# A gated cross-attention and quantized feed-forward kernel: earlier dequantization, a softmax in large steps, later transposes

## The chip, the cores and the metric

The kernel runs on one core of a Trainium2 chip. The core has a matrix engine (TensorE, PE in the profile, with its weight loads shown as PEld), a vector engine (DVE), a scalar engine (ACT), GpSimd (POOL) and SyncE (SP), which here only issues DMAs. Each engine works through its own instruction stream in order, and semaphores hold an instruction until what it needs is there. The metric is the device time of one execution in microseconds (us). Three runs of the kernel before took 1498.82, 1499.34 and 1502.29 us; the median is 1499.34 us.

## The reference

The input x has 4 sequences of 1024 tokens of 512 numbers; a context has 4 x 64 tokens. Cut to what is computed:

```
x = x + tanh(g_xattn) * attention(layernorm(x), ctx)      # 16 heads of 64, 64 keys,
                                                          # keys after the token's position get -10000
h = act_qdq(layernorm(x))                                 # rounded to 16 bits by one scale over all of h
up   = act_qdq(h @ dequant(w_up).T)                       # 1536 columns
gate = act_qdq(h @ dequant(w_gate).T)
sig  = round(sigmoid(gate) * 65536) / 65536
gate = act_qdq(gate * sig)
o    = act_qdq(gate * up)
x = x + tanh(g_ffn) * (o @ dequant(w_down).T)
```

act_qdq divides by the largest magnitude of the whole tensor, so each of these four scales needs all of its tensor before the first element can be rounded. dequant works on blocks of 32 weights: the largest magnitude of a block divided by 7 is its scale, the weights are divided by it, rounded and multiplied again. All arithmetic is float32.

## The kernel before, in words

The 4096 tokens are 32 tiles of 128 (t = 0 to 31). A tile scheduler orders the instructions of DVE, ACT, POOL and SP by their place in the program and by when it expects them to be ready, and may move one forward where its engine would be idle; `high_priority(SOON)` makes an instruction count as 150 places earlier, and `keep_in_program_order` forbids moving it. In the large stages PE's order is written out by hand (`manual_schedule`). Twenty buffers of 8 KB per partition (`slot`, NS = 20) are shared by everything large.

**Setup (0 to 79 us).** The weights of the attention are loaded and folded: `m_all` (query and key weights with the context, one matrix per sequence) and `vwo` (value and output weights with the context). `score_sums(0)` (L358) makes the sums of `m_all` that a seven-product form of the score multiplication uses: four DVE additions of 128x1024 (L368 to L373). It stands before the loop that makes `vwo` (L509), whose results go from PSUM to SBUF by ACT (L522) and DVE (L524).

**Attention (79 to 588 us).** The loop over pairs of tiles q calls `scores(q + 1)` and `softmax(q + 1)` one pair ahead, and then `attend(t)` for its two tiles. `softmax` takes the maximum of each head (L590, 128x1024), negates it (L591), runs 16 exponentials on ACT, one a head, with the maximum as bias and the sum collected beside it (L594), and multiplies by the reciprocal sum (L599, L600). `attend` transposes the weights on PE (L614), calls `then()`, which does `renormed(t - 4)` (the second layer norm, L636 to L644) and, in the second half, prepares one of twelve 128-row chunks of the gate weights, and multiplies with `vwo` (L620, 16 matmuls). `gate_chunk` (L239) for chunk oc comes at tile 16 + oc * 16 // 12, that is at 16, 17, 18, 20, 21, 22, 24, 25, 26, 28, 29 and 30. It loads the chunk (L208, SP), dequantizes it with six DVE instructions (L211 to L220; `dequantized`), transposes it with four PE instructions (L225) and copies it to `wgT` on ACT (L228; `turned`). Its raw buffers are two. The first DVE instruction of chunks 0 and 1 is kept in program order. From tile 24 on, eight chunks of the up weights are dequantized as well (`w_eu`), and from tile 26 on sums of `wgT` are made (L288 to L291).

**Gate products (590 to 885 us).** 24 units v, each of 28 matmuls in seven products (m1, m5, m2, m6, m7, m4, m3 of `unit_steps`), interleaved so that the last three steps of a unit run among the first four of the next. The gate results go to DRAM (`gate_d`). The down weights are loaded and dequantized here (`wd`).

**Up products (885 to 1181 us).** 24 more units, `at` = 0 to 23, of 12.0 us each. Beside them `gate_integers(n)` turns gate results that are loaded back (`load_gates`, L938, 1 MB a pair) into integers: for each of 48 half units three ACT instructions (L968, L969, L971), one DVE instruction (L973) and a store on SP (L974). `products` multiplies magnitudes (L994 on ACT, L995 on DVE) to find the place of the largest product. After the loop the first operands of the last stage are asked for (`load_early(0)`, L1085, 1 MB and 0.5 MB), the place of the largest product is found and its row read (L1105), and then, in PE's written order, four transposed chunks of the down weights (`down_turned`, each four transposes L225 and one ACT copy L228), m7, three more, m4, m3, and the last five. `half_of_last` takes in the halves of the last unit as they come (L980, L984, L985). Two more `load_early` follow.

**Down products (1197 to 1499 us).** First the two scales (`up` and `o`) are made by a chain of short DVE and POOL instructions (L184 to L203), and a flag `full` (L1162) is read by every engine for a branch (L1165, L1166) around a fallback that does not run. Then `integers` makes the operands: an ACT instruction (L1193), L1197 and L1202 on DVE. PE does 96 matmuls for the first block of tokens (L1344), then the seven-product form for the others (L1267), to the end.

Of the kernel before, what the change touches and what calls it, by code (L numbers as in the profile page):

```python
# [27 lines left out]
def kernel(  # L28
# [71 lines left out]
    SOON = 150  # L100
    NQ = NT // 2
    QPB = TPB // 2

    xf = x.flatten_outer_dims()
    of = out.flatten_outer_dims()
# [97 lines left out]
            nc.vector.tensor_scalar(inv, inv, unit, None, ALU.mult)  # L203
        return s, inv

    def dequantized(pool, src, w, name, in_order=False):
# [4 lines left out]
        ins = nc.vector.tensor_reduce(am, wb, AX.X, ALU.max, apply_absolute_value=True)  # L211
        if in_order:
            tc.keep_in_program_order(ins)
# [6 lines left out]
        nc.vector.tensor_tensor(wb, wb, am.unsqueeze(2).to_broadcast(shape), ALU.mult)  # L220

    def turned(ps, w, dst, in_order=False):

        for j in range(4):
            ins = nc.tensor.transpose(ps[:, j, :], w[:, j * P : (j + 1) * P], ident)  # L225
            if in_order:
                tc.keep_in_program_order(ins)
        nc.scalar.copy(dst, ps)  # L228

    def weight_chunk(pool, psp, src, dst, name, in_order):  # L230
        w = pool.tile([P, H], F32, name=f"w_{name}", tag="wraw")
        dequantized(pool, src, w, name, in_order)
        turned(psp.tile([P, 4, P], F32, name=f"wps_{name}", tag="tr"), w, dst)

    wgT, wuT, wd, wdT, up_chunks = [], [], [], [], []

    def gate_chunk(pool, psp, oc):  # L239
        if oc % 4 == 0:  # L240
            wgT.append(slot([P, HC, 4 * P], f"wgT{oc // 4}"))
        cols = slice((oc % 4) * P, (oc % 4 + 1) * P)
        weight_chunk(
            pool, psp, w_gate[oc * P : (oc + 1) * P, :], wgT[-1][:, :, cols], f"g{oc}", oc < 2
        )

    def up_chunk(psp, w, in_order=False):

        oc = len(up_chunks)
        up_chunks.append(oc)  # L250
        if oc % 4 == 0:
            wuT.append(slot([P, HC, 4 * P], f"wuT{oc // 4}"))
        cols = slice((oc % 4) * P, (oc % 4 + 1) * P)
        ps = psp.tile([P, 4, P], F32, name=f"wps_u{oc}", tag="tr")
        turned(ps, w, wuT[-1][:, :, cols], in_order)

    def down_chunk(pool, k):
        if k % 4 == 0:
# [117 lines left out]
    with tc.tile_pool(name="su", bufs=1) as su, tc.tile_pool(  # L376
# [122 lines left out]
        for b in range(2, B):  # L499
            for k in range(2):  # L500
                nc.gpsimd.dma_start(out=m_d[b][k], in_=m_all[b][k])
        for _ in score_sums(0):
            pass


        for b in range(B):
            vwo.append([slot([P, HP // 2, H], f"vwo{b}_{n}") for n in range(2)])
        load_group(1)
        for a in reversed(range(B // 2)):  # L509
            for hp in range(HP):  # L510
                for b in (2 * a, 2 * a + 1):
                    ps = ps_mm.tile([P, H], F32, name=f"ps_vo{b}_{hp}", tag="mm")
                    for j in range(2):
                        half = slice(j * D, (j + 1) * D)
                        to = j if b % 2 == 0 else 1 - j
                        nc.tensor.matmul(
                            ps[to * D : (to + 1) * D, :], vT[half, hp, b * KL : (b + 1) * KL],
                            wo[hp // 4][half, hp % 4, :], start=True, stop=True,
                        )
                    dst = vwo[b][hp // 4][:, hp % 4, :]  # L520
                    if b % 2 == 0:
                        nc.scalar.copy(dst, ps)  # L522
                    else:
                        nc.vector.tensor_copy(dst, ps)  # L524
                    if b > 1 and hp % 4 == 3:
                        nc.gpsimd.dma_start(out=vwo_d[b][hp // 4], in_=vwo[b][hp // 4])
# [3 lines left out]
    with tc.tile_pool(name="ps_s", bufs=1, space=PSUM) as ps_s, tc.tile_pool(  # L530
# [48 lines left out]
        def softmax(q, e):  # L579

            for i in range(2):
                t = 2 * q + i
                ei = e[:, i]

                if t % TPB == 0:
                    nc.vector.tensor_tensor(
                        ei, ei, cmask.unsqueeze(1).to_broadcast([P, NH, KL]), ALU.add
                    )
                mx = pa.tile([P, NH], F32, name=f"mx{t}", tag="mx")
                nc.vector.tensor_reduce(mx, ei, AX.X, ALU.max)  # L590
                nc.vector.tensor_scalar(mx, mx, -1.0, None, ALU.mult)  # L591
                sm = pa.tile([P, NH], F32, name=f"sm{t}", tag="sm")
                for h in range(NH):
                    nc.scalar.activation(  # L594
                        ei[:, h, :], ei[:, h, :], AF.Exp, bias=mx[:, h : h + 1],
                        accum_out=sm[:, h : h + 1],
                    )
                rs = pa.tile([P, NH], F32, name=f"rs{t}", tag="rs")
                nc.vector.reciprocal(rs, sm)  # L599
                nc.vector.tensor_tensor(  # L600
                    ei, ei, rs.unsqueeze(2).to_broadcast([P, NH, KL]), ALU.mult
                )
# [51 lines left out]

        sg_t, ag, early_up = [], [], []
        last = NT - GRP
        half = NT // 2
        group_stats(pa, 1)
        rstd_of(pa, [(rstd1[:, of_group(1)], mv1[:, of_group(1), 1])], "a1")

# [7 lines left out]
        for q in range(NQ):  # L668
# [19 lines left out]
            for i in range(2):  # L688
                t = 2 * q + i

                def between():
                    if q > 1:
                        renormed(t - GRP)
                    if t >= half:
                        for oc in range(IC):
                            if t - half == oc * (NT - half) // IC:
                                gate_chunk(pa, ps_tr, oc)

                attend(t, e, between)
                if t >= NT - UPB:  # L700
                    ag.append(weight_sums(wgT, sg_t, t - (NT - UPB), "g"))

# [30 lines left out]
    with tc.tile_pool(name="praw", bufs=RAW) as praw, tc.tile_pool(  # L733
# [184 lines left out]
        with tc.tile_pool(name="pc", bufs=2) as pc, tc.tile_pool(  # L918
# [27 lines left out]
            def up_done(r, v, k):  # L946
# [6 lines left out]
                queue = nc.sync if v == order[-1] else nc.scalar  # L953
                queue.dma_start(out=up_d[u], in_=raw[u])

            gsi = {}
            made = []

            def gate_integers(n):


                for j in range(len(made), min(n, NU)):
# [67 lines left out]
            gates = {v: load_gates(v) for v in order[:3]}  # L1030
            for at, v in enumerate(order):
                tp, p = divmod(v, UPB)
                if p == UPB // 2 and at + UPB < NV:
# [39 lines left out]
                if at > 0:  # L1073
# [8 lines left out]
            def load_early(k):  # L1082
                up, gs = slot([P, 2, UW], f"upe{k}"), slot([P, 2, UW], f"gse{k}", I16)
                for dst, src in ((up, up_d), (gs, gsi_d)):
                    nc.sync.dma_start(  # L1085
                        out=dst, in_=src[2 * k : 2 * k + 2].rearrange("u p w -> p u w")
                    )
                return up, gs
# [312 lines left out]
```

## Time and profile before

| what | value |
|---|---|
| median of three runs | 1499.34 us |
| the profiled execution | 1501.24 us |
| its span, first to last instruction | 1499.4 us |
| PE busy | 1445.4 us, 96% |
| DVE busy | 1086.1 us, 72% |
| ACT busy | 643.4 us, 43% |
| POOL busy | 70.8 us, 5% |
| mean granted TensorE clock | 0.990 |
| mean DMA rate | 155 GB/s |

How to read it: a line of the view of waits says which engine and line waited for which, with the total, the number of times and the longest. A line of the timeline gives the start, the duration, the engine and line, output <- inputs, the shape, the number of instructions taken together and, in brackets, how long the engine had been idle and what ended that. A line of the view of stretches gives, for each stretch, the busy time of the engines (with the number of instructions), the granted TensorE clock as a share of full speed, the mean busy share of the DMA engines and their rate. The profiled execution lies 1.9 us above the median of the runs, and 1.84 us of its time lie outside its span.

### The profile page before, as it was taken

Reading aid. Unit: us, or ns where it says so; the run is one execution under the profiler, and the core shown is the slowest. Engines: PE = TensorE matmul, PEld = TensorE weight load, DVE = VectorE, ACT = ScalarE, POOL = GpSimd, SP = SyncE. Lnnn points to the kernel's source line nnn. Section 1 sums busy time; section 2 is a strip of 40 time slices with the busy share of each in tenths; the row PEclk is TensorE's granted clock in tenths of the full one; section 3 lists DMA queues with packets and bytes.
Section 4 is the critical chain, followed back from the end, with each engine's and each line's share of the span. In section 5 each row is a group of like instructions: output and inputs, shape, how many; then the busy total and the mean of one; then the engine's idle time right before and its main releaser. Section 6 shows DMA issues by size and latency. Waiting matters only on the chain. (4 is left out here: it accounts for less than half of the span.)

```text
span 1499.4 us, 14520 instructions
## 1 busy us (share of the span) xinstructions
PE 1445.4 (96%) x4656; PEld 797.1 (53%) x4656; DVE 1086.1 (72%) x1984; ACT 643.4 (43%) x1715; POOL 70.8 (5%) x143
## 2 busy tenths in 40 slices
PE   8989999998999989999999999999999599999999
PEld 6544445444454545444444444444444248888887
DVE  2865657649577887999856558888888797666642
ACT  2455645665456654110000127777787532222200
POOL 0100000000000001000000000000000101111110
PEclk9999999999999999999999999999999899999999
DMA  7521221302122144743322528868583585554321
GB/s 280 221 89 43 78 78 60 141 21 82 57 84 85 36 162 153 282 176 155 126 84 85 178 88 309 334 203 324 207 338 135 183 313 206 182 183 169 140 71 43
DMA packets 71477, 231.69 MB, mean 155 GB/s; under 512 B 7268, under 2 KB 7524, under 8 KB 65892
## 3 DMA queue, kind: packets, MB, share of 16 engines
q1 hardware_dynamic: 46212, 131.09, 24.8%
q0 software_dynamic: 11648, 50.34, 8.7%
q10 hardware_dynamic: 13536, 49.29, 8.2%
q8 instruction: 37, 0.61, 0.2%
q14 instruction: 44, 0.36, 0.1%
HBM read 123.74 MB, written 106.95 MB: 154 GB/s over the span
## 5 line engine op out<-in xcount | busy, mean ns | idle before, releaser
L594 ACT ACTIVATE e<-e,mx 128x64 f32<-128x64 f32 x512 | 170.2, 337 | 14.7 <-DVE mx L591 14.6
L620 PE MATMUL po<-vb,eT 128*128 128x512 f32 x256 | 116.2, 608 | 0.9 <-ACT eT L616 0.9
L620 PE MATMUL po<-vwo,eT 128*128 128x512 f32 x256 | 114.8, 601 | 2.0 <-ACT eT L616 1.7
L594 ACT ACTIVATION_READ_ACCUMULATOR e<-e,mx 128x1 f32 x512 | 97.3, 190 | 0.0
L756 PE MATMUL pqup<-t,wuT 128*128 128x512 f32 x192 | 91.8, 600 | 2.1 <-DVE raw_up L777 0.9
L756 PE MATMUL pqgate<-t,wgT 128*128 128x512 f32 x192 | 90.4, 593 | 0.0
L620 PEld LDWEIGHTS po<-vb,eT 128*128 128x128 f32 x256 | 48.9, 196 | 57.3 <-issue 55.6
L620 PEld LDWEIGHTS po<-vwo,eT 128*128 128x128 f32 x256 | 47.7, 191 | 58.8 <-issue 53.9
L1193 ACT ACTIVATE uie<-upe,inv_up 128x1024 int16<-128x1024 f32 x48 | 53.7, 1145 | 58.4 <-DVE upe L1197 34.3
L772 ACT COPY raw_gate<-ppgate 128x512 f32<-128x512 f32 x24 | 14.0, 585 | 147.8 <-PE ppgate L756 147.8
L1267 PE MATMUL ep<-wdT,upe 128*128 128x256 f32 x336 | 77.1, 379 | 0.0
L1267 PE MATMUL eq<-tw,upe 128*128 128x256 f32 x312 | 72.5, 379 | 0.2 <-DVE c L1289 0.2
L1267 PEld LDWEIGHTS ep<-wdT,upe 128*128 128x128 f32 x336 | 63.8, 190 | 9.1 <-issue 0.5
L552 DVE TENSOR_TENSOR e<-sq,e 128x512 f32<-128x512 f32 x48 | 33.0, 688 | 47.9 <-PE sq L546 47.9
L756 PE MATMUL ppup<-xu,wuT 128*128 128x512 f32 x144 | 67.7, 592 | 0.0
L756 PE MATMUL ppgate<-xh,wgT 128*128 128x512 f32 x144 | 67.7, 592 | 0.0
L1197 DVE SCALAR_TENSOR_TENSOR upe<-uie,inv_o,gse 128x1024 f32<-128x1024 int16 (+1 forms) x50 | 60.8, 1241 | 9.3 <-ACT uie L1193 4.0
L973 DVE SCALAR_TENSOR_TENSOR q<-gi,inv_gs,si 128x1024 int16<-128x1024 int16 x48 | 60.6, 1278 | 5.0 <-ACT si L971 4.9
L1267 PEld LDWEIGHTS eq<-tw,upe 128*128 128x128 f32 x312 | 59.1, 190 | 8.7 <-DVE c L1289 0.6
L756 PEld LDWEIGHTS pqup<-t,wuT 128*128 128x128 f32 x192 | 35.1, 190 | 51.4 <-issue 34.4
L756 PEld LDWEIGHTS pqgate<-t,wgT 128*128 128x128 f32 x192 | 36.2, 190 | 46.4 <-issue 38.5
L884 DVE TENSOR_REDUCE am_gate<-raw_gate 128x1 f32<-128x1024 f32 x48 | 58.2, 1213 | 0.9
(323 smaller groups left out, 2833.8 us busy)
## 6 DMA issues: line engine op xcount, KB each, us to landing
gate_d<-raw_gate ACTq DMA_DIRECT2D x48, 512.0 KB, 2.6
gt<-gate_d SPq DMA_DIRECT2D x48, 512.0 KB, 6.2
upe<-up_d SPq DMA_DIRECT2D x24, 1024.0 KB, 6.2
up_d<-raw_up ACTq DMA_DIRECT2D x46, 512.0 KB, 4.8
gsi_d<-q SPq DMA_DIRECT2D x48, 256.0 KB, 4.1
gse<-gsi_d SPq DMA_DIRECT2D x24, 512.0 KB, 4.8
xg<-in_x_dram SPq DMA_DIRECT2D x8, 1024.0 KB, 5.3
x_d<-xg POOLq DMA_DIRECT2D x32, 256.0 KB, 2.3
```

Source lines behind the costliest of these rows:

```text
L552: nc.vector.tensor_tensor(dst, bank[at], other, add)
L594: nc.scalar.activation(ei[:, h, :], ei[:, h, :], AF.Exp, bias=mx[:, h : h + 1], accum_out=sm[:, h : h + 1],)
L620: nc.tensor.matmul(po, eT[:, hp, :], vwo[b][hp // 4][:, hp % 4, :], start=(hp == 0), stop=(hp == HP - 1),)
L756: nc.tensor.matmul(bank[at], a[k][:, h, :], b[k][:, h, :], start=start and h == 0, stop=h == HC // 2 - 1, skip_group_check=True,)
L772: nc.scalar.copy(r0[:, 0, :], bank["pp"])
L884: nc.vector.tensor_reduce(am_gate[:, u : u + 1], rf, AX.X, ALU.max, apply_absolute_value=True)
L973: nc.vector.scalar_tensor_tensor(gsi[u], gi, c_gs, si, ALU.mult, ALU.mult)
L1193: nc.scalar.activation(ui, up[:, i, :], AF.Copy, scale=inv_u)
L1197: ins = nc.vector.scalar_tensor_tensor(o[:, i, w], ui[:, w], c_o, gs[:, i, w], ALU.mult, ALU.mult)
L1267: nc.tensor.matmul(bank[at], a[u // 2][k][:, u % 2, q % 2, :], w_of[u // 2][k][:, u % 2, :], start=start and u == 0, stop=u == UPB - 1, sk ...
```

## The change

- `score_sums(0)` is emitted between the two halves of the loop that makes `vwo`.
- For the first pair of tiles (q = 0) the softmax subtracts the maximum with one DVE instruction of 128x1024, takes one ACT exponential of 128x1024 and sums with one DVE reduction of 128x1024, in place of the negation and the 16 exponentials. The other 15 pairs are as before.
- A gate chunk is loaded and dequantized after the `attend` that lies three tiles before the one in which it is transposed, in four raw buffers. No instruction of it is kept in program order any more.
- `gate_integers` runs further ahead in the last units. The number of half units made by the end of unit `at` goes from 2 at + 4 to 2 at + 4 + 2 (at - 17): 42 by unit 18, 46 by unit 19 and all 48 by unit 20, where it was 40, 42 and 44, and 48 by unit 22. Gate loads are asked for correspondingly earlier. The last four integer results go to a slot of their own (`last_q`).
- The three `load_early` are emitted with unit 22, with unit 23 and after the row loads; two of their 16-bit operands share a slot.
- Of the twelve transposed chunks of the down weights one comes before m7, one after it, and ten after m3.
- The ACT instruction L984 of `half_of_last` gets the high priority.

```diff
-        for _ in score_sums(0):
-            pass
...
         for a in reversed(range(B // 2)):
+            if a == 0:
+                for _ in score_sums(0):
+                    pass
...
                 mx = pa.tile([P, NH], F32, name=f"mx{t}", tag="mx")
                 nc.vector.tensor_reduce(mx, ei, AX.X, ALU.max)
-                nc.vector.tensor_scalar(mx, mx, -1.0, None, ALU.mult)
                 sm = pa.tile([P, NH], F32, name=f"sm{t}", tag="sm")
-                for h in range(NH):
-                    nc.scalar.activation(
-                        ei[:, h, :], ei[:, h, :], AF.Exp, bias=mx[:, h : h + 1],
-                        accum_out=sm[:, h : h + 1],
+                if q == 0:
+
+                    nc.vector.tensor_tensor(
+                        ei, ei, mx.unsqueeze(2).to_broadcast([P, NH, KL]), ALU.subtract
                     )
+                    nc.scalar.activation(ei, ei, AF.Exp)
+                    nc.vector.tensor_reduce(sm, ei, AX.X, ALU.add)
+                else:
...
+        gate_at = [NT // 2 + oc * (NT // 2) // IC for oc in range(IC)]
+        gate_raw = {}
...
-                    if t >= half:
-                        for oc in range(IC):
-                            if t - half == oc * (NT - half) // IC:
-                                gate_chunk(pa, ps_tr, oc)
+                    if t in gate_at:
+                        oc = gate_at.index(t)
+                        turned_chunk(ps_tr, gate_raw.pop(oc), oc, wgT, "g")
 
                 attend(t, e, between)
+                if t + AHEAD in gate_at:
+                    oc = gate_at.index(t + AHEAD)
+                    w = pa.tile([P, H], F32, name=f"w_g{oc}", tag="wraw", bufs=4)
+                    dequantized(pa, w_gate[oc * P : (oc + 1) * P, :], w, f"g{oc}")
+                    gate_raw[oc] = w
...
-                    gsi[u] = pc.tile([P, UW], I16, name=f"q{u}", tag="q", bufs=5)
+                    if j < NU - 4:
+                        gsi[u] = pc.tile([P, UW], I16, name=f"q{u}", tag="q", bufs=5)
+                    else:
+                        if j == NU - 4:
+                            last_q.append(slot([P, 4, UW], "last_q", I16))
+                        gsi[u] = last_q[0][:, j - NU + 4]
...
-                nc.scalar.activation(ar, r, AF.Abs)
+                with tc.high_priority(SOON):
+                    nc.scalar.activation(ar, r, AF.Abs)
...
-                    gate_integers(2 * at + min(4, at // 4))
-                    if at + 2 < NV:
-                        gates[order[at + 2]] = load_gates(order[at + 2])
+
+                    late = max(0, at - (NV - UPB - 1))
+                    soon = max(0, at + 1 - (NV - UPB - 1))
+                    gate_integers(2 * at + min(4, at // 4) + 2 * late)
+                    for v in order[len(gates_loaded) : at + 3 + 2 * soon]:
+                        gates_loaded.append(v)
+                        gates[v] = load_gates(v)
+                    if at + 2 >= NV:
+                        load_early()
...
-            early = [load_early(0)]
...
+            load_early()
+
             turn = down_turned(ps_tr)
-            for _ in range(4):
-                next(turn)
+            next(turn)
             half_of_last(0, 0)
-            for step, half, n in zip(tail, ((1, 1), (0, 1), (1, 0)), (3, 0, 5)):
+            for step, half, n in zip(tail, ((1, 1), (0, 1), (1, 0)), (1, 0, IC - 2)):
                 step()
                 half_of_last(*half)
                 for _ in range(n):
                     next(turn)
-            for k in range(1, UPB // 2):
-                early.append(load_early(k))
```

More of the change, by code (lines that the diff above doesn't have):

```diff
@@ L102 @@
     QPB = TPB // 2
+    AHEAD = 3
     xf = x.flatten_outer_dims()
@@ L204, in act_scale, with dequantized @@
         return s, inv
-    def dequantized(pool, src, w, name, in_order=False):
+    def dequantized(pool, src, w, name):
         nc.sync.dma_start(out=w, in_=src)
@@ L210, in dequantized @@
         am = pool.tile([P, NQB], F32, name=f"wam_{name}", tag="wam")
-        ins = nc.vector.tensor_reduce(am, wb, AX.X, ALU.max, apply_absolute_value=True)
-        if in_order:
-            tc.keep_in_program_order(ins)
+        nc.vector.tensor_reduce(am, wb, AX.X, ALU.max, apply_absolute_value=True)
         nc.vector.tensor_scalar(am, am, 1.0 / W_QMAX, 1e-12, ALU.mult, ALU.max)
@@ L220, in dequantized, with turned, turned_chunk, up_chunk @@
         nc.vector.tensor_tensor(wb, wb, am.unsqueeze(2).to_broadcast(shape), ALU.mult)
-    def turned(ps, w, dst, in_order=False):
+    def turned(ps, w, dst):
         for j in range(4):
-            ins = nc.tensor.transpose(ps[:, j, :], w[:, j * P : (j + 1) * P], ident)
-            if in_order:
-                tc.keep_in_program_order(ins)
+            nc.tensor.transpose(ps[:, j, :], w[:, j * P : (j + 1) * P], ident)
         nc.scalar.copy(dst, ps)
[L230 to L233, printed above, removed]
     wgT, wuT, wd, wdT, up_chunks = [], [], [], [], []
-    def gate_chunk(pool, psp, oc):
+    def turned_chunk(psp, w, oc, into, name):
         if oc % 4 == 0:
-            wgT.append(slot([P, HC, 4 * P], f"wgT{oc // 4}"))
+            into.append(slot([P, HC, 4 * P], f"w{name}T{oc // 4}"))
         cols = slice((oc % 4) * P, (oc % 4 + 1) * P)
[L243 to L247, printed above, removed]
+        ps = psp.tile([P, 4, P], F32, name=f"wps_{name}{oc}", tag="tr")
+        turned(ps, w, into[-1][:, :, cols])
+    def up_chunk(psp, w):
         oc = len(up_chunks)
         up_chunks.append(oc)
[L251 to L255, printed above, removed]
+        turned_chunk(psp, w, oc, wuT, "u")
     def down_chunk(pool, k):
@@ L590, in softmax @@
                 nc.vector.tensor_reduce(mx, ei, AX.X, ALU.max)
-                nc.vector.tensor_scalar(mx, mx, -1.0, None, ALU.mult)
                 sm = pa.tile([P, NH], F32, name=f"sm{t}", tag="sm")
-                for h in range(NH):
-                    nc.scalar.activation(
-                        ei[:, h, :], ei[:, h, :], AF.Exp, bias=mx[:, h : h + 1],
-                        accum_out=sm[:, h : h + 1],
-                    )
+                if q == 0:
+                    nc.vector.tensor_tensor(
+                        ei, ei, mx.unsqueeze(2).to_broadcast([P, NH, KL]), ALU.subtract
+                    )
+                    nc.scalar.activation(ei, ei, AF.Exp)
+                    nc.vector.tensor_reduce(sm, ei, AX.X, ALU.add)
+                else:
+                    nc.vector.tensor_scalar(mx, mx, -1.0, None, ALU.mult)
+                    for h in range(NH):
+                        nc.scalar.activation(
+                            ei[:, h, :], ei[:, h, :], AF.Exp, bias=mx[:, h : h + 1],
+                            accum_out=sm[:, h : h + 1],
+                        )
                 rs = pa.tile([P, NH], F32, name=f"rs{t}", tag="rs")
@@ L656 @@
         last = NT - GRP
-        half = NT // 2
+        gate_at = [NT // 2 + oc * (NT // 2) // IC for oc in range(IC)]
+        gate_raw = {}
         group_stats(pa, 1)
@@ L954, in up_done, with load_early @@
                 queue.dma_start(out=up_d[u], in_=raw[u])
+            early = []
+            def load_early():
+                k = len(early)
+                up = slot([P, 2, UW], f"upe{k}")
+                if k % 2 == 0:
+                    early_gs.append(slot([P, 2, 2, UW], f"gse{k}", I16))
+                gs = early_gs[-1][:, k % 2]
+                for dst, src in ((up, up_d), (gs, gsi_d)):
+                    nc.sync.dma_start(
+                        out=dst, in_=src[2 * k : 2 * k + 2].rearrange("u p w -> p u w")
+                    )
+                early.append((up, gs))
+            early_gs, last_q = [], []
             gsi = {}
@@ L1029 @@
             tokens = {done_last: b}
-            gates = {v: load_gates(v) for v in order[:3]}
+            gates_loaded = order[:3]
+            gates = {v: load_gates(v) for v in gates_loaded}
             for at, v in enumerate(order):
@@ L1077 @@
                     products(order[at - 1])
-                    gate_integers(2 * at + min(4, at // 4))
-                    if at + 2 < NV:
-                        gates[order[at + 2]] = load_gates(order[at + 2])
[L1082 to L1088, printed above, removed]
-            early = [load_early(0)]
+                    late = max(0, at - (NV - UPB - 1))
[6 more added lines that the diff above has]
+                        load_early()
             first = over_all([am_p], "first")
```

## The prediction

> **What bounds the kernel now.** I began with the page's busy times.
>
> ```profile
> PE 1445.4 (96%) x4656; PEld 797.1 (53%) x4656; DVE 1086.1 (72%) x1984; ACT 643.4 (43%) x1715; POOL 70.8 (5%) x143
> ```
>
> PE is the bound; no edit removes one of its products. What can be won is its 54 us of idle time (1499.4 - 1445.4), and what each pause costs afterwards. So next came PE's own waits.
>
> ```profile
> PE ps_d L1344 <- DVE upe L1202: 13.0, 1, 13.0
> PE wps_g L225 <- DVE w_g L220: 12.2, 2, 6.8
> ...
> PE ps_e L614 <- DVE e L600: 3.1, 1, 3.1
> PE po L620 <- ACT eT L616: 2.6, 9, 0.5
> PE wps_d L225 <- ACT wdT L228: 2.6, 4, 1.8
> PE ps_vo L516 <- DVE vwo L524: 2.3, 3, 0.9
> ```
>
> All but one of these lie where the change works: the end of the up products, two gate chunks, the first softmax, the copies of `vwo`. Then the timeline, for the price after a pause:
>
> ```profile
> 109.01 1.94 PE L614 MATMUL ps_e<-ident,e 128*128 128x128 f32 x8 [3.06 <-DVE e L600]
> ...
> 110.78 7.76 PE L620 MATMUL po<-vwo,eT 128*128 128x512 f32 x16
> ...
> 356.74 1.09 PE L225 MATMUL wps_g<-ident,w_g 128*128 128x128 f32 x4 [6.77 <-DVE w_g L220]
> ...
> 357.62 8.84 PE L620 MATMUL po<-vb,eT 128*128 128x512 f32 x16
> ...
> 368.07 7.03 PE L620 MATMUL po<-vb,eT 128*128 128x512 f32 x16
> ```
>
> The same 16 products take 7.03 us without a pause and 8.84 after one. The stretches show why: the granted clock is halved.
>
> ```profile
> 355.00:360.00 5.00, 3.26 (x7) 1.93 (x8) 4.97 (x14) 5.00 (x32) 0.00 (x0) 0.50 0.21 56
> ```
>
> Of 5 us PE is busy 3.26, PEld 1.93, DVE 4.97, ACT 5.00, POOL 0; then the clock, 0.50, the DMA share and the rate. So a removed pause brings its length and its aftermath.
>
> Last, the timeline behind the last up product:
>
> ```profile
> 1179.38 1.88 PE L756 MATMUL pnup<-b,su 128*128 128x512 f32 x4
> ...
> 1184.55 0.59 ACT L228 COPY wdT<-wps_d 128x512 f32<-128x512 f32 x1 [0.26 <-PE wps_d L225]
> ...
> 1188.38 0.22 DVE L1162 SCALAR_TENSOR_TENSOR full<-a_ends,other_end,below 128x1 int32<-128x1 f32 x1
> ...
> 1192.56 3.23 ACT L1193 ACTIVATE uie<-upe,inv_up 128x1024 int16<-128x1024 f32 x3 [7.42 <-DMA upe<-up_d]
> ```
>
> The product ends at 1181.26, its scales are ready at 1188.6, ACT starts at 1192.56, 4.0 after the flag, and PE at 1197.54. The chain of waits names DVE from there to 1258, then PE to the end, so what moves ACT's start moves the end.
>
> **Sums of `m_all` (L368 to L373), moved.** Four instructions of 1.22, 4.9 us of DVE, now fill 58.4 to 63.7, in front of the first `vwo` copies. PE's waits on those copies are 2.3, and 0.9 more at the first score product. Behind half of them the sums may still be moved forward into the same gap. Ends: 3.2 gained; 2.5 lost, half of the 4.9 falling between copies with five PSUM buffers as cover. I take 1.0 gained.
>
> **First softmax.** Per tile a negation (0.17) and 16 exponentials (0.33 apart) go; a subtraction (as L600, 1.22), an exponential (as L971, 128x1024, 1.05) and a sum (as L590, 1.17) come. The first maximum is ready at 96.1. Then 1.22, the table load 1.28, 1.05, 1.17, 0.25 (L599) and 1.22 (L600) end at 102.3; the second maximum and the L552 of the next scores lie between, 1.17 + 3 x 0.69, so about 105.5. It was 108.87, and PE wants it at 105.95. The pause of 3.06 goes, and its aftermath: 1.94 - 1.04 on the transposes and 7.76 - 7.03 on the products, 4.7 in all. DVE gets 2 x (1.22 + 1.17 - 0.17) = 4.4 more in a stretch where it is busy 17.1 of 25, so a new wait of 1 is likely. Ends: 4.7 and 0 (if the second tile's 2.4 goes first); I take 3.7.
>
> **Gate chunks.** A chunk is 0.68 + 0.17 + 0.25 + 0.69 + 0.42 + 0.69 = 2.9 us of DVE; its number is unchanged. Tiles 16 to 30 take 208.8 us (357.62 to 566.39 in L620), 14.9 each, so three tiles earlier is some 45 us earlier. Chunk 0, tile 16: the wait of 6.77 goes, and 8.84 - 7.03 and 1.09 - 0.63 behind it: 9.0. Chunk 10, tile 29: a wait of 5.40 and 8.54 - 7.03 and 0.46: 7.4. Late next: at tile 17 the `xm` that DVE makes at 357.65, which PE would want at 358.4, but 5.8 us of chunks 0 and 1 no longer stand before it; at tile 30 the weights whose L600 ends at 552.6, which PE would want at 557. The cover is DVE's free time; at 475 to 500 it is busy 24.89 of 25. The density there stays (gate chunks 9 to 11 replace 7 to 9), so I take off 0.4: 16.0 gained. Ends: 16.4; 9.0, if the second wait is only handed on.
>
> On SP a chunk's load stands behind x and `m_all` loads; with four buffers its buffer is free since the tile five or six before. A new danger: chunks 0 and 1 were loaded at 17.49 already, landing after up to 12.2, but their first DVE instruction was held. Now four chunks are free to go ahead, and DVE, in order, would stand at a load. If that is in front of the copy L460 at 24.77, four landings to about 31 (0.25 MB each at 347 GB/s) and one chunk's 2.9 make 34, 9.4 lost, with 1.6 of slow clock 11. Other end: 3 gained, from work taken off tiles 16 to 20. Nearest row: the ten chunks that were not held cost DVE 2.9 for loads altogether. I take 1.0 lost.
>
> **Gate integers ahead.** Units 18 and 19 each get two half units more: on ACT 2 x (1.14 + 1.14 + 1.05) = 6.7, where it is busy about 9.6 of 12.0 (19 to 21 of 25 in the stretches there). So 4.3 too much, twice, until units 21 and 22, which have none. DVE gets 2.6 on 10.5. Queued behind L968 on ACT are the copies L764 and L772, which PE waits for. SP's stores and loads keep their number; the last gate load is already issued at 1106.6, in unit 18. Ends: 8.6 lost; 0.5 gained by ease later. Nearest row: from 625 to 700 DVE is full and PE does not wait. I take 1.0 lost.
>
> **Behind the last product.** Of seven transposed chunks ahead of m3 two stay: 20 transposes at 0.13 are 2.6, the waits there are 2.95. So m3 could end 5.5 earlier; DVE must still take up m7 (L782) before m4, about 1, so 4.5. L973 no longer stands there (2 x 1.28 off DVE). L984 ahead of the copies saves 0.35. Against: ten chunks then follow, on ACT two each 1.45 apart; five ended 3.9 after m3, ten end 7.5 after, at 1184.3, and the flag comes at 1183.8: 0.5 lost. The `load_early` move before the row load on SP; the third follows it. The 3 MB that fill the DMA engines from 1185 to 1193 go, while ACT passes the branch in 4.0; at the first branch, with the DMA at a fifth, it took 2.3. Ends: 8 gained (with 1.7 of that and the DVE order, L1197 ahead of L1202 by 1.28); 2 lost, if a load holds SP in front of the row load. I take 4.5.
>
> A rule against it: the transposes now stand where PE is otherwise idle. Here the clock is 1.00 until 1186, two microseconds after the last transpose and five after the last product, so the row cannot say which counts. The Trainium skill, "TensorE: Matmul & The Clock Gate", Part 4: PE-mode transpose, says that transposes do not count as PE activity in the same way. By it half of the ten chunks would run at half clock, the copies would end some 2 us later, and this part would be 2.5, the total 2 us more.
>
> **Sum.** -1.0 - 3.7 - 16.0 + 1.0 + 1.0 - 4.5 = -23.2. The profiled execution took 1501.24 (span 1499.4), so 1478.0; from the median, 1499.34, it is 1476.1. I take 1477.
>
> **Rivals.**
> - *Start block* (above): 10 more than I took, 1487. For it, the loads at 17.49; against, DVE's gaps of 3.2 between 31 and 43, in which a chunk fits. 0.13.
> - *The second gate wait handed on* in the full stretch of DVE: 7 more, 1484. For it 24.89 of 25; against, the 5.8 that leave 545 to 562. 0.12.
> - *ACT the bound in units 18 to 20*: 7.6 more, 1485. 0.12.
> - *Nothing won behind the last product*, ACT's copies or the branch taking the 4.5: 1481.5. 0.10.
> - *Slower: every chunk waits for its load.* SP, in order behind a held x load, issues each load only as DVE reaches it; DVE stands 2.8 (median landing) and PE with it, 5.7 with the chunk's 2.9. It outweighs 23.2 + 4.5 from five chunks on; at eight it is 45.6, so 1523. For it, two such waits now (2.9 in all); against, the 45 us ahead. Eight chunks 0.08; four, which give 1500, 0.04.
> - The forecast itself: 0.41.
>
> **How the numbers follow.** About 0.3%, 4.5 us, is what a measurement here can tell from no change. Slower 0.08; the same 0.04; faster 0.88, the forecast and four rivals. Since several of these could meet, I move 0.03 from faster to each side: 0.82, 0.07, 0.11. The low end is all best ends of the known parts, -3.2 - 4.7 - 16.4 - 8 = -32, softened by the 2 of likely cost: 1469. The high end takes in the start block and one further rival: 1494.
>
> **What the new profile would show.** The waits on `w_g` and on L600 gone, the clock at 1.00 at 355 and 555 and its drop at 110 gone; L211 of chunk 0 far ahead of tile 13 and no DVE wait at 25; ACT full without PE waiting in units 18 to 20; m3 about 4.5 sooner relative to its unit, and ACT's first L1193 as much. Wrong it would be by a DVE wait for `w_g` before 50 us, by a wait on `raw_up` after 1090, or by ACT's copies ending after the flag.

## The result, and the profile after

The changed kernel takes 1495.37 us (median; 1494.09 to 1496.3) against 1499.6 for the kernel before in the same comparison: a ratio of 0.9969, 95% interval 0.996 to 0.9979. It is 4.2 us faster, where 23 were forecast, and lies 1.4 above the top of the range. The profiled execution took 1494.27 us, its span is 1492.5 (1499.4 before). The two spans differ by 6.9 and not by 4.2, because the profiled execution before lies 1.6 above the median of its runs and the one after 1.1 below. Lines have moved: the copy L460 is now L447, L600 is L596, L764 is L766, L994 is L1018, L984 is L1008, L1193, L1197 and L1202 are L1213, L1217 and L1222. The kernels made from it for the experiments are up to three lines off again; there the names behind the line tell which instruction it is.

The page's busy times after. The work is the same, PE's idle time is 48.0 us in place of 54:

```profile
PE 1444.5 (97%) x4656; PEld 795.4 (53%) x4656; DVE 1087.2 (73%) x1986; ACT 635.6 (43%) x1653; POOL 70.5 (5%) x143
```

The view of waits after, PE's own:

```profile
PE ps_m L465 <- DVE wqT L447: 15.4, 1, 15.4
...
PE ps_d L1364 <- DVE upe L1222: 4.5, 1, 4.5
PE ppup L758 <- ACT raw_up L766: 4.0, 1, 4.0
...
PE ps_vo L504 <- DVE vwo L512: 1.9, 3, 0.6
...
PE ps_e L610 <- DVE e L596: 0.6, 1, 0.6
```

What the prediction saw go is gone or smaller: the 12.2 for the gate weights are gone, the 3.1 for the first softmax are 0.6, the 13.0 before the down products 4.5. Two waits are new, 15.4 at the start and 4.0 in the up products. The stretches of the two old gate waits, and of the new one at 1125, show the granted clock (the figure behind POOL's count; 0.86 in the first two before):

```profile
350.00:375.00 25.00, 24.88 (x88) 13.12 (x87) 24.06 (x54) 15.45 (x58) 1.08 (x2) 1.00 0.25 91
550.00:575.00 25.00, 24.76 (x91) 13.22 (x90) 23.70 (x64) 15.94 (x68) 1.63 (x3) 1.00 0.16 56
1125.00:1150.00 25.00, 21.74 (x46) 9.36 (x47) 20.66 (x26) 22.34 (x24) 0.00 (x0) 0.93 0.50 179
```

To see where the time went I set the starts of the same PE rows side by side in the two timelines, and took the difference from one landmark to the next:

| from, to | start of the last row (end for the flag), before, after | step | forecast |
|---|---|---|---|
| span start, first `vwo` product | 60.72, 76.91 | +16.2 | +1.0 |
| to the first score product (sums of `m_all`) | 79.31, 95.57 | +0.1 | -1.0 |
| to the second tile's transposes (softmax) | 118.37, 131.14 | -3.5 | -3.7 |
| to the last tile's transposes (gate chunks) | 573.26, 569.67 | -16.4 | -16.0 |
| to m2 of the last up unit (gate integers) | 1163.85, 1166.78 | +6.5 | +1.0 |
| to m3 of the last up unit | 1179.38, 1177.60 | -4.7 | -4.5 |
| to the flag `full` | 1188.60, 1186.84 | 0.0 | 0 |
| to the first down product | 1197.54, 1190.40 | -5.4 | 0 |
| to the end of the span | 1499.4, 1492.5 | +0.2 | 0 |
| sum | | -6.9 | -23.2 |

The start, first the copy of `wqT` in the timeline before, then the same stretch after:

```profile
24.77 1.29 DVE L460 COPY wqT<-ps_wq 128x512 f32<-128x512 f32 x2 [17.39 <-PE ps_wq L456]
```

```profile
29.67 0.69 DVE L212 TENSOR_REDUCE wam_g<-w_g 128x16 f32<-128x512 f32 x1 [22.35 <-DMA w_g<-in_L_ffn_w_gate_dram]
...
38.87 0.69 DVE L219 TENSOR_TENSOR w_g<-w_g,wam_g 128x512 f32<-128x512 f32 x1
39.48 1.28 DVE L447 COPY wqT<-ps_wq 128x512 f32<-128x512 f32 x2
40.31 3.48 PE L465 MATMUL ps_m<-kT,wqT 64*128 64x256 f32 x16 [15.40 <-DVE wqT L447]
```

DVE stands from 7.3 to 29.67 at the load of a gate chunk that is not wanted before tile 16, then makes four chunks (24 instructions, 9.8 us), and only then the copy that PE has wanted since 24.9. The first 16 products after it take 3.48 instead of 2.00, as the granted clock is 0.50 from 29.70 to 43.35.

Tile 16, where PE waited 6.77 and took 8.84 for the 16 products:

```profile
362.61 0.66 PE L224 MATMUL wps_g<-ident,w_g 128*128 128x128 f32 x4
363.10 7.03 PE L616 MATMUL po<-vb,eT 128*128 128x512 f32 x16
```

The up products, ACT's and PE's rows in order of time:

```profile
1111.87 2.19 ACT L986 ACTIVATE gi<-gt,inv_gate 128x1024 int16<-128x1024 f32 x2
...
1119.53 2.34 ACT L986 ACTIVATE gi<-gt,inv_gate 128x1024 int16<-128x1024 f32 x2 [0.93 <-DVE q L996]
...
1125.75 1.99 ACT L1018 ACTIVATE ar<-raw_up 128x1024 f32<-128x1024 f32 x2
...
1127.65 0.56 ACT L766 COPY raw_up<-ppup 128x512 f32<-128x512 f32 x1
1128.26 3.30 PE L758 MATMUL ppup<-xu,wuT 128*128 128x512 f32 x4 [3.96 <-ACT raw_up L766]
```

Four half units (two from 1111.87, two from 1119.53) stand on ACT in front of the magnitudes L1018. These two read the raw buffers of unit 18, and the copy L766 of unit 20 writes into one of them. So m2 of unit 20 waits 3.96, and 1.9 more go in slow products (3.30 and 2.31 for 1.88 and 1.88, the clock at 0.50 from 1128.79 to 1132.20).

Behind the flag, in the timeline after:

```profile
1186.62 0.22 DVE L1182 SCALAR_TENSOR_TENSOR full<-a_ends,other_end,below 128x1 int32<-128x1 f32 x1
...
1187.81 4.38 ACT L1213 ACTIVATE uie<-upe,inv_up 128x1024 int16<-128x1024 f32 x4 [1.29 <-SPq L1186]
...
1188.99 0.75 DVE L1217 SCALAR_TENSOR_TENSOR upe<-uie,inv_o,gse 128x512 f32<-128x512 int16 x1 [0.91 <-ACT uie L1213]
...
1189.78 0.52 DVE L1222 TENSOR_SCALAR upe<-upe 128x512 f32<-128x512 f32 x1
...
1190.40 10.00 PE L1364 MATMUL ps_d<-wdT,upe 128*128 128x512 f32 x19 [4.50 <-DVE upe L1222]
```

From the flag to the first down product it is 3.56 now, 8.94 before. The view of the branch's line of the kernel *before* shows that the prediction misread that time:

```profile
L1166 DVEq COMPARE_BRANCH  x1: 63/63/63, 1189.0 to 1189.0; - x1
...
L1166 ACTq COMPARE_BRANCH  x1: 45/45/45, 1193.0 to 1193.0; - x1
```

DVE took the branch at 1189.0, ACT at 1193.0, *after* the start of its first L1193 at 1192.56. So that L1193 stands in front of the branch in ACT's stream, and ACT did not need 4.0 to pass the branch: it stood for something in front of it, and in the changed kernel the first L1213 starts 1.0 after the flag.

What it stood for is in the trace's semaphore updates, and it is not what the bracket of the row names (a load of `upe`). ACT's wait went on until 1192.32. The one semaphore of its list that was completed just then, at 1192.30, is that of the last store of `raw_up`, the second L954 of SP:

```profile
1180.33 0.37 SPq L954 DMA_DIRECT2D up_d<-raw_up  x1
1180.75 1.62 SPq L1085 DMA_DIRECT2D upe<-up_d  x1
1182.41 0.46 SPq L954 DMA_DIRECT2D up_d<-raw_up  x1
```

It was issued behind a load of 1 MB and took 9.9 to land. In the changed kernel the two stores are issued together, at 1181.21 and 1181.68, with no load between or in front, and have landed by 1185.2. Why L1193 waits for that store is not shown; that its output lies in memory which the raw buffers had is likely.

### The profile page after: what moved, and what is told of

Its sections match the earlier page's. It is cut to its first block, busy times and chain, and to the rows that moved or that the text cites. A ratio compares the mean times of both kernels' runs of the same rounds, so it can differ in the third digit from the quotient of the medians.

```text
span 1492.5 us, 14450 instructions
## 1 busy us (share of the span) xinstructions
PE 1444.5 (97%) x4656; PEld 795.4 (53%) x4656; DVE 1087.2 (73%) x1986; ACT 635.6 (43%) x1653; POOL 70.5 (5%) x143
## 5 line engine op out<-in xcount | busy, mean ns | idle before, releaser
L590 ACT ACTIVATE e<-e,mx 128x64 f32<-128x64 f32 x480 | 159.6, 337 | 17.9 <-DVE mx L588 17.8
L616 PE MATMUL po<-vb,eT 128*128 128x512 f32 x256 | 112.9, 594 | 0.8 <-ACT eT L612 0.8
L590 ACT ACTIVATION_READ_ACCUMULATOR e<-e,mx 128x1 f32 x480 | 91.6, 191 | 0.0
L1213 ACT ACTIVATE uie<-upe,inv_up 128x1024 int16<-128x1024 f32 x48 | 53.6, 1144 | 50.5 <-DVE upe L1217 31.5
L1217 DVE SCALAR_TENSOR_TENSOR upe<-uie,inv_o,gse 128x1024 f32<-128x1024 int16 (+1 forms) x50 | 60.5, 1237 | 5.3 <-ACT uie L1213 5.3
L996 DVE SCALAR_TENSOR_TENSOR q<-gi,inv_gs,si 128x1024 int16<-128x1024 int16 x44 | 55.7, 1277 | 4.8 <-ACT si L989 4.7
```

The lines of the kernel that those rows point to most:

```text
L590: nc.scalar.activation(ei[:, h, :], ei[:, h, :], AF.Exp, bias=mx[:, h : h + 1], accum_out=sm[:, h : h + 1],)
L616: nc.tensor.matmul(po, eT[:, hp, :], vwo[b][hp // 4][:, hp % 4, :], start=(hp == 0), stop=(hp == HP - 1),)
L1213: nc.scalar.activation(ui, up[:, i, :], AF.Copy, scale=inv_u)
L1217: ins = nc.vector.scalar_tensor_tensor(o[:, i, w], ui[:, w], c_o, gs[:, i, w], ALU.mult, ALU.mult)
```

## The experiments

Each comparison is with the kernel before on the same chip. Steps are the differences of the table, against the kernel before.

**The gate chunks held again.** Only the hold comes back; loads, buffers and place stay.

```diff
-        nc.vector.tensor_reduce(am, wb, AX.X, ALU.max, apply_absolute_value=True)
+        ins = nc.vector.tensor_reduce(am, wb, AX.X, ALU.max, apply_absolute_value=True)
+        if in_order:
+            tc.keep_in_program_order(ins)
...
-                    dequantized(pa, w_gate[oc * P : (oc + 1) * P, :], w, f"g{oc}")
+                    dequantized(pa, w_gate[oc * P : (oc + 1) * P, :], w, f"g{oc}", oc < 4)
```

> The changed kernel with one thing put back: the first DVE instruction of the first four gate chunks is kept in program order; their loads stay at 17.5 us and the four buffers stay. Theory A (DVE's order): the four chunks, 9.8 us of DVE behind a landing at 29.67, stood in front of the copy of ps_wq. The wait of 15.4 goes, the first score product comes at 79.3 instead of 95.57, and the time is 1495.4 - 16.3 = 1479; up to 3 more if the 10 us of DVE work now meet tiles 13 to 16. Theory B (the loads): 1 MB asked for at 17.5 us keeps the DMA engines from what the start needs. The loads are where they were, so the first score product stays within 5 us of 95.6 and the time above 1490.

1481.52 us, ratio 0.9874 (0.9854 to 0.9893). The timeline:

```profile
23.96 1.29 DVE L449 COPY wqT<-ps_wq 128x512 f32<-128x512 f32 x2 [16.74 <-PE ps_wq L445]
24.80 2.00 PE L467 MATMUL ps_m<-kT,wqT 64*128 64x256 f32 x16 [0.44 <-DVE wqT L449]
```

The copy is back at 24, with the four loads where they were: theory A, and B falls. The start's step goes from +16.2 to -0.8. Two amounts are given back: 2.1 more in the up products, 1.2 of it because the same stall of 3.96 has a longer slow clock behind it (6.83 us in place of 3.41; 3.78 and 3.01 for the next two rows), and 3.0 between tiles 8 and 16, where a wait of 2.8 for `xn` has come:

```profile
PE ps_xn L335 <- DVE xn L323: 3.4, 2, 2.8
```

**The kernel before without its hold.** One argument goes:

```diff
-            pool, psp, w_gate[oc * P : (oc + 1) * P, :], wgT[-1][:, :, cols], f"g{oc}", oc < 2
+            pool, psp, w_gate[oc * P : (oc + 1) * P, :], wgT[-1][:, :, cols], f"g{oc}", False
```

> The kernel before with one thing taken out: the first DVE instruction of gate chunks 0 and 1 is no longer kept in program order; two buffers, everything else as it was. Theory A (whatever gate chunk has a free buffer at the start goes in front of the copy of ps_wq on DVE, and the price is its landing plus the DVE time of all of them): two chunks, landing at 29 to 29.7, then 2 x 2.45, so the copy comes at 34 to 35 instead of 24.77: 9.8 later at the first score product. Chunk 0 is then ready long before tile 16, so the wait of 6.77 there and 2.3 behind it go: -9.1. Time 1499.6 + 0.7 = 1500.3. Rival B (only the four buffers and the place three tiles ahead make the planner move them): nothing moves, the copy stays at 24.8 and the time at 1499.6 with the wait at tile 16 in place. Rival C (the prediction's price, one chunk of 2.9 behind the landing): 7 later at the first score product.

1503.8 us, ratio 1.0026 (1.0014 to 1.0037). DVE's rows:

```profile
29.65 0.69 DVE L211 TENSOR_REDUCE wam_g<-w_g 128x16 f32<-128x512 f32 x1 [22.31 <-DMA w_g<-in_L_ffn_w_gate_dram]
...
34.66 1.28 DVE L460 COPY wqT<-ps_wq 128x512 f32<-128x512 f32 x2
```

The copy is 9.9 late (24.77 before), the first score product 11.7 with the slow clock, and the step at tile 16 is -9.1: theory A, whose 9.8 left that clock out. (Of the 3.5 above its 1500.3 the clock is 1.9; 0.7 in the up products and 0.9 behind the first down product are not explained.) Two chunks go in front because two buffers are free, four with four buffers. The hold kept the start clear, and the wait at tile 16 was its price.

**The gate integers at the pace of before.**

```diff
-                    late = max(0, at - (NV - UPB - 1))
-                    soon = max(0, at + 1 - (NV - UPB - 1))
+                    late = soon = 0
```

> The changed kernel with the gate integers and their loads at the pace of before (late = soon = 0). Theory A (four half units in a row on ACT, 1111.9 to 1125.8, stand before the two L1018 that free the buffer which the copy of m1 of unit 20 needs): the wait of 4.0 and the slow clock behind it go, 5.9 to 6.5 us by unit 23; two late half units then put 2.6 us of DVE and 6.7 of ACT in front of the last products, so half of the 4.7 won up to m3 is lost: 1495.4 - 6.2 + 2.4 = 1491.6. Rival B (the early loads or the higher priority of the last magnitudes disturb unit 20): the wait stays, 1495 or more. Rival C (the pace is what wins the whole tail): m3 and the first down product lose all of their 10: 1499.

1491.69 us, ratio 0.9941 (0.9921 to 0.9961). The step in the up products is -0.2 in place of +6.5. ACT has two half units between the pairs of magnitudes, and the copy follows them in time:

```profile
1119.90 1.99 ACT L1018 ACTIVATE ar<-raw_up 128x1024 f32<-128x1024 f32 x2
1121.79 0.57 ACT L766 COPY raw_up<-ppup 128x512 f32<-128x512 f32 x1
```

What it costs came elsewhere than expected: m3 keeps its 4.6, but from the start of m3 to the flag it is 12.2 instead of 9.2, as DVE makes the products of the unit before, and ACT the last magnitudes, only behind the two late integers. So the added pace costs 6.5 and brings 3.0. (This run's start was 1.5 worse than the changed kernel's, 17.7. That the time is theory A's 1491.6 is partly luck: it had the wait right and the price of the late integers in the wrong place.)

**The pace kept, the magnitudes made urgent.**

```diff
-                nc.scalar.activation(ar, raw[u], AF.Abs)
+                with tc.high_priority(SOON):
+                    nc.scalar.activation(ar, raw[u], AF.Abs)
```

> The changed kernel with one thing added: the magnitudes L1018 of the products get the high priority on ACT, at the full pace of the integers. Theory A (the copy of m1 of unit 20 waited because the two L1018 that free its buffer stood behind four half units of integers): without that the copy comes in time, the wait of 4.0 and the slow clock go, 5.5 to 6.5 less by unit 23: 1495.4 - 6 = 1489.4. Rival B (four half units, 13.4 us of ACT in one unit of 12, are simply too much, whatever their order): a wait of 2 to 4 stays in units 19 to 21, 1493 to 1496. Rival C (magnitudes taken early stand in front of the copies instead, as they wait for DVE): new waits on raw_up all along, over 1496.

1499.92 us, ratio 0.9999 (0.9988 to 1.0011): all of the gain lost, and my theory with it. The wait of 4.0 is gone, but the step is +10.9:

```profile
PE pqup L758 <- DVE raw_up L779: 9.1, 7, 2.7
...
PE ppup L758 <- ACT raw_up L766: 2.5, 3, 1.7
```

There are seven waits on the sums that DVE makes from the copies, where there were three of 1.7 in all, and three on the copy. On ACT the magnitudes now stand for DVE's results 25 times, where it was 8 times and 12.6 us:

```profile
ACT ar L1019 <- DVE raw_up L944: 29.5, 25, 3.0
```

That is rival C. Which two instructions came late was right; that their order alone was the cause was not. With chunks held and made four tiles ahead, the full pace and the same priority gave 1482.55 us (0.9882, 0.986 to 0.9904), with the up step at +11.1: rival C again.

> The held kernel with chunks four tiles ahead, the full pace of the integers, and the high priority for the magnitudes L1018. Theory A (the priority takes the wait out of unit 20 and the pace keeps what it gives behind m3): 1474.2 - 3.0 = 1471.2. Rival B (ACT too full whatever the order): the up stage loses 2 to 6, 1473 to 1477. Rival C (the magnitudes now stand in front of the copies all along): over 1477.

**The early loads where they were.** `load_early` is called once behind the loop and twice behind the transposes, as before.

```diff
-                    if at + 2 >= NV:
-                        load_early()
...
+            load_early()
             first = over_all([am_p], "first")
...
+            for _ in range(1, UPB // 2):
+                load_early()
```

> The changed kernel with the three early loads asked for where they were before: one behind the last unit, two behind the last transposes. Theory A (before, ACT stood 4.0 us behind the flag at the landing of upe, and DVE 2.4 more at that of gse): both come back, the first down product 5 us later relative to the flag, 1495.4 + 5.2 = 1500.6. Rival B (the prediction's reading: 4.0 is the passing of the branch, slowed by busy DMA engines, 1.7 to be won): 1497.1. Rival C (the order of L1217 and L1222 on DVE gave the gain, whatever the loads do): under 1496.5.

1497.1 us, ratio 0.9983 (0.9973 to 0.9992), which is the number of rival B, but not for its reason: SP's rows show the first load at 1143.4 all the same, moved forward by the scheduler. So it was run again with the DMAs held on SP:

```diff
-                    nc.sync.dma_start(
-                        out=dst, in_=src[2 * k : 2 * k + 2].rearrange("u p w -> p u w")
-                    )
+                    tc.keep_in_program_order(
+                        nc.sync.dma_start(
+                            out=dst, in_=src[2 * k : 2 * k + 2].rearrange("u p w -> p u w")
+                        )
+                    )
```

> The changed kernel with the three early loads where they were before, as in the earlier run, and their six DMAs kept in program order on SP, so that none can be moved forward to 1143 us. Theory A (the early loads are what the first instruction of the last stage on ACT waits for): ACT starts its first L1213 at 1191 to 1193 and the first down product comes at 1195 to 1197, 5 us behind the changed kernel: 1500.5. Rival B (they land in time, and only the order of L1217 and L1222 on DVE costs): 1.2 behind, 1497.

1497.89 us, ratio 0.999 (0.9977 to 1.0003). From the flag, at 1187.79, to the first down product it is 5.19:

```profile
1187.37 2.19 ACT L1215 ACTIVATE uie<-upe,inv_up 128x1024 int16<-128x1024 f32 x2
...
1189.85 1.15 ACT L1215 ACTIVATE uie<-upe,inv_up 128x1024 int16<-128x1024 f32 x1 [0.29 <-DMA upe<-up_d]
...
1191.26 1.28 DVE L1219 SCALAR_TENSOR_TENSOR upe<-uie,inv_o,gse 128x1024 f32<-128x1024 int16 x1 [1.30 <-DMA gse<-gsi_d]
```

ACT's first two need not wait, the third waits 0.29, and DVE takes a full L1219 that waits 1.30 for `gse` in front of the L1224 that PE wants. The loads' place alone is worth 1.6 of the 5.4, nearer to rival B's 1.2; theory A, 5 us, falls. In this run SP issues the two last stores of `raw_up` together at 1182.35, ahead of the loads, and they have landed by 1186.9, before ACT comes to its first L1215. So the late store of the kernel before has not come back. The other 3.8 are read from the semaphores of two traces, and no experiment on the changed kernel brings them back. (The kernel before without its hold shows the late store again: it is complete at 1195.55, and the first L1193 starts at 1195.80.)

**The transposes in the order of before.**

```diff
-            next(turn)
+            for _ in range(4):
+                next(turn)
             half_of_last(0, 0)
-            for step, half, n in zip(tail, ((1, 1), (0, 1), (1, 0)), (1, 0, IC - 2)):
+            for step, half, n in zip(tail, ((1, 1), (0, 1), (1, 0)), (3, 0, 5)):
```

> The changed kernel with the transposed down chunks in the order of before: four ahead of m7, three more ahead of m4, five behind m3. Theory A (the transposes and the waits for their copies stand in front of m7, m4 and m3): m3 comes 4.7 us later relative to its unit, the flag with it, and the time is 1495.4 + 4.7 = 1500.1. Rival B (the two half units of integers that left the tail made 2.6 of the 4.7, and the copies behind m3 give back 0.5): 1495.4 + 1.6 = 1497. On the clock: if transposes keep it up, its drop follows the last transpose by 3 to 4 us; if only products do, it falls 6 to 11 us behind the last product.

1498.64 us, ratio 0.9985 (0.9975 to 0.9995). m3 keeps 2.4 of its 4.7. With the pace undone instead it kept 4.6, with both parts it is 4.7: either part alone covers much of the same wait, so their prices do not add up. Rival B had this half right. (Up to m3 this run loses 2.3 against the changed kernel; the start and the up products, which the edit does not touch, were 2.2 worse in the profiled execution.) The last two stores of `raw_up` are 2.0 apart again, as before, but no load goes out between them: the second lands 2.6 after its issue, and the first down product comes 3.80 behind the flag. So neither the old place of the loads nor the old order of the transposes brings the late store by itself.

**The last magnitudes without priority.**

```diff
-                with tc.high_priority(SOON):
-                    nc.scalar.activation(ar, r, AF.Abs)
+                nc.scalar.activation(ar, r, AF.Abs)
```

> The changed kernel without the high priority of the last four magnitudes L1008 (L984 before the change). Theory A (the prediction's 0.35: one copy of 0.58 less in front of a magnitude): the flag comes 0.35 later behind m3, the rest as it was, 1495.7. Rival B (the priority makes what the other three parts of the tail don't, some 3 us of the 10): the first down product comes 3 later, 1498. Rival C (the planner puts them where they were anyway): 1495.4, no row moved.

1495.18 us, ratio 0.9969 (0.9959 to 0.9978), the same as with it. From m2 of the last unit to m3 the step is -4.7, to the first down product -5.4: this part of the change does nothing (rival C).

**Both repairs, and one more.** Held chunks and the pace of before:

> The changed kernel with both repairs: the first four gate chunks held in program order, and the gate integers at the pace of before. Theory A (the two are independent): the up stage gives back its 8.6 of the held kernel to within 0.3, the last stage loses 3.0 between m3 and the first down product, so 1481.5 - 8.6 + 3.0 = 1476. Rival B (the up stage loses whatever the pace, because the held chunks or the earlier start shift its loads): 1479 to 1482.

1478.33 us, ratio 0.9858 (0.9834 to 0.9882). The up products' step is +0.3 and the two repairs are independent; but between tiles 8 and 16 it loses 4.7, with the same wait of 2.84 for `xn`: here the clock is at 0.50 for 3.41 us behind it (345.10 to 348.52), in the held kernel it was not. Then the chunks four tiles ahead (`AHEAD = 4`), which puts none beside tiles 15, 19 and 23, where DVE makes the group statistics:

> As the kernel with both repairs, and the gate chunks made four tiles ahead in place of three, so that none is made beside the group statistics of tiles 15, 19 and 23. Theory A (the wait of 2.84 for xn at 344.7 came from chunk 2 in the middle of the statistics chain on DVE): that wait goes, 3.0 less, 1473. Rival B (held chunks cost DVE 2.9 each wherever they stand among tiles 12 to 16): the wait only moves, 1476.

1474.24 us, ratio 0.9834 (0.981 to 0.9859). The step between tiles 8 and 16 is 0.0: theory A. Last, the same with half the added pace, 45 half units by unit 20 and 48 by unit 21:

> The held kernel with chunks four tiles ahead, and the integers at half the added pace: 45 half units by unit 20, all 48 by unit 21. Theory A (three half units are 10 us of ACT beside 3.3 of copies and magnitudes, 1.3 too much in each of two units, which the slack of 2 us before m2 takes up; with no integers left behind unit 22 the 3.0 between m3 and the first down product come back): 1474.2 - 3.0 + 0.5 = 1471.7. Rival B (one unit too full is enough for the wait on the copy of m1): 3 to 4 lost in unit 21 or 22, 1474 to 1475.

1475.76 us, ratio 0.9833 (0.9812 to 0.9854). From the start of m3 to the flag it is 9.2 again, so the 3.0 come back, and four microseconds are lost before, rival B's amount, though only 0.5 of it is a wait on a copy and the longest wait, 2.1 in the last unit, is for a sum of DVE:

```profile
PE pqup L760 <- DVE raw_up L781: 4.0, 3, 2.1
```

Neither pace is better than the other; 1474 to 1476 us is the best that was run, 25 us under the kernel before.

## Why the prediction was wrong

- **Gate chunks, -16.0; measured -16.4.** Right by its steps: tile 16 gave 9.1 (9.0 forecast), tile 29 7.1 (7.4), with 0.2 over for the rest. The clock is at 1.00 in both stretches. The rival that hands the second wait on did not come, nor did the slower one: PE waited for no chunk, and DVE stood 2.4 for two later loads.
- **Softmax, -3.7; measured -3.5.** The wait of 3.06 became 0.65, as DVE made the row 2.4 sooner; the rest is the clock.
- **Sums, -1.0; measured +0.1.** The waits on the `vwo` copies went from 2.3 to 1.9, but the stretch took 18.7 in place of 18.6: PE won nothing by it.
- **Start danger, +1.0; measured +16.2. This is the step that failed.** The mechanism stood in the prediction, with its place and its sign of recognition; its size and its chance were wrong. The bound took four landings to about 31 and one chunk's 2.9, which make 34. The landing was earlier, 29.67, but all four chunks went in front of the copy, 9.8 us and not 2.9: 29.67 + 9.8 = 39.5, the 39.48 of the trace, and the first product was 1.5 longer on the slow clock. And the row taken as the nearest, ten unheld chunks that cost DVE 2.9 for loads, was the wrong one: those were asked for from 357.86 on, when DVE had other work to do. The row that bore on it was the pair at 17.49 with DVE idle for 17 us before 24.77. The scheduler put every chunk that had a free buffer into that idle time. Both kernels without the hold give the same price: the landing plus the work of as many chunks as have buffers, 29.67 + 9.8 for four and 29.65 + 5.0 for two.
- **Gate integers, +1.0; measured +6.5.** The rival "ACT the bound in units 18 to 20" came, near the end of 8.6 given for it, and in the named instruction, the copy behind L968. The row taken as nearest, DVE full while PE does not wait, is of another engine and another queue. The link that was not seen is that the copy waits for a raw buffer which the magnitudes free, and these stand behind the integers.
- **Behind the last product, -4.5; measured -10.1.** m3 came 4.7 sooner, for the 4.5 forecast, and from m3 to the flag nothing changed, as counted. The 5.4 behind the flag were not in the sum. "ACT passes the branch in 4.0" was the failed reading: ACT stood in front of the branch, for a store that SP had issued behind a load, and the view of the branch's line showed before the change that ACT had not reached it. The high end of 8 held 3.0 of it, as L1197 ahead of L1202 and a faster branch.

The two costs met, 20.7 us over their terms, and 5.6 more than forecast came from the end. The rival "start block" priced alone was 1487; with ACT's rival beside it, 7.6 more, it would have been 1494.6 by the prediction's own prices; 1495.4 was measured. That this comes so close is luck: the start cost 5 more than that rival's price, and the gain behind the flag, which was in no sum, made up for it.

## What to carry to other kernels

A hold on program order is a part of the kernel like any other: before it is dropped, ask which idle gap the freed instruction can reach, and price it as the landing it would wait for plus the work of every sibling that has a buffer. Work that is moved forward on an engine with slack in the mean still delays what stands behind it; follow what that frees, buffers too, to the one that waits. Before a pause beside a branch is put down to the branch, look whether the engine has reached it, and which semaphore ended its wait: it may be a store that was issued behind a large load.

## What the runs showed of the hardware

The transposes kept the clock up. In the kernel before, the products end at 1181.3 and the transposes at 1184.5; in the changed one at 1179.5 and 1185.9. The stretches of one microsecond show the clock falling at 1187.3 before:

```profile
1187.00:1188.00 1.00, 0.00 (x0) 0.00 (x0) 0.94 (x7) 0.00 (x0) 0.31 (x2) 0.64 1.03 401
```

and at 1190.2 after:

```profile
1190.00:1191.00 1.00, 0.60 (x1) 0.50 (x2) 0.96 (x3) 1.00 (x1) 0.57 (x2) 0.61 0.68 197
```

That is 2.8 and 4.3 behind the last transpose, but 6.0 and 10.8 behind the last product. With the transposes in the order of before it is 2.6 and 5.9. For comparison, in pauses behind products the clock fell 2.7 after the start of the pause (108.67, before) and 4.5 (1128.79, after). So 10.8 is too late for the products to have held it alone. What the Trainium skill says in "TensorE: Matmul & The Clock Gate", Part 4: PE-mode transpose, that transposes do not count as PE activity in the same way, and what the prediction made of it, 2 us more, does not hold for these float32 transposes: the measurement decides. Whether they run in the mode that the page means is not shown.

What a pause of PE costs beyond its length follows the clock and not the length. In these traces a stretch at 0.50 between two at 1.00 lasts 3.41 us or 2, 3, 4 or 5 times that. The same wait of 3.96 cost 5.9 in the changed kernel, with 3.41 us at 0.50, and 7.1 in the held one, with 6.83; the same wait of 2.84 cost 3.0 without a slow stretch and 4.7 with one. The longest pause, 15.4 where 0.4 stood before, cost 16.2: only the part of its slow stretch in which PE worked again, 3.0 us, counts.
